# Loading the second layer's weight matrices in 192 KB pieces into fixed places

## Chip, cores and metric

The kernel runs on one core of one Trainium2 chip. The metric is the device time of one execution in microseconds (us); shown are the single runs and their median. The page and the trace come from one further, profiled execution.

## The reference, cut to what matters

Two graph layers follow each other on 128 graphs of 64 nodes with 768 features, in float32. The weights of the second layer, Wq, Wk, Wv and Wf, are what the change concerns.

```python
x = _layernorm(x + _L0_gnn_ref(x, adj, W, b, w_src, w_dst, H_w, H_b))       # 12 heads of 64
x = _layernorm(x + _L1_gnn_ref(x, Wq, bq, Wk, bk, Wv, bv, Wf, bf, adj))     # 6 heads of 128

# _L0_gnn_ref: h = x @ W per head; th = tanh(h)
attn = leaky(th @ w_src + (th @ w_dst).T)        # masked by adj, softmax over nodes
feat_out = elu(attn @ h + b)
gate = sigmoid(x @ H_w.T + H_b)
return gate * feat_out + (1.0 - gate) * x

# _L1_gnn_ref
q, k, v = heads(x @ Wq + bq), heads(x @ Wk + bk), heads(x @ Wv + bv)
probs = softmax(q @ k.T / sqrt(128) + bias_of(adj))
return (probs @ v) @ Wf + bf
```

## The kernel before, in words

**Products.** Every multiplication by a 768 x 768 matrix is done as a two by two block product with seven block multiplications instead of eight. Each matrix is therefore held as seven blocks of 384 x 384: W11, W21, W22, T1, T2, T3 and N4, of which four are sums and differences of weights. One matrix in SBUF is a tile of 128 partitions, seven blocks, KH = 3 slices of the contracted dimension, and 384 columns; a block is 576 KB, the matrix 4.1 MB. The products take the blocks in the order of TURNS (line 64): W11, T2, T1, W21, T3, W22, N4. `by_token` (line 274) gives tokens as rows, with the weights as the moving operand: h, g (the gate), v and o. `by_feature` (line 345) gives features as rows: q and k, 256 tokens at a time for each of 7 products.

**First layer.** The 64 token tiles of 128 are taken in 32 pairs (loop at line 794). For each pair `hidden` multiplies by w0, `gate` by h_w, and `value` by wv, the last for the pair two before. That is 21 products, one period. The rest of a tile's work (`attend`, line 574) runs over the two periods from its start: scores, softmax, a DMA transpose of the weights (`turn_weights`, line 667), whose result ACT puts together (`weights`, line 671), 24 small matmuls on each side of the graph pair (`means`, line 674, tile f_all), elu and gate, layer norm, a second DMA transpose (`turn_rows`, line 731), whose result ACT puts together (`rows`, line 735, tile x_even or zone), and sums of the transposed rows (line 749, x_sums), which `value` reads. The blocks of rows go to device memory (`away`, line 762) as operands of the second layer, and v too (line 541).

**Second layer.** `phase_b` goes through 16 quads of four tiles. For each of three f it makes queries and keys (`by_feature`), and starts `slab` (line 888), which does the scores and the softmax of two heads, turns the result by a DMA transpose (line 936, tiles s and sT; ACT copies at lines 935 and 940), multiplies by v (tile c_ps, line 952), and turns that by two more DMA transposes (line 967). `output` multiplies by wf. `last_bias` (line 854) also reads wf, before the first keys of quad 1.

**Order of work.** The kernel has a schedule of its own: class `Beat` (line 94) counts products. `product` emits one product and moves the count by one; `at` queues a piece of work for a count, `start` runs a generator whose yields are numbers of beats to wait, and `until` lets the count run on. Keys in `KEYS`, `SUMS`, `X_BLOCKS` and `MASKS` say at which beat of the period each step of `attend` and its neighbours is emitted. Emission order is the order on each engine's queue. All DMAs, transposes included, are issued by SP on one queue, in order; an SP instruction that waits holds all behind it.

**The matrices.** w0, h_w and wv are loaded at the start (`prepared`, line 187). Meanwhile `matrices` (line 437) builds the seven blocks of wq, wk and wf and writes them to device memory (`to_there`, line 209). `matrix` (line 222) brings one back: it takes the next buffer of the pool `weights` (line 169, three buffers), so that wq takes the one of w0, wk that of h_w and wf that of wv, and issues seven DMAs of 576 KB, one a beat; then it sets `ready`. In the last pair (period of 21 beats from its beat 0) wq starts behind `hidden`, wk behind `gate`. After the loop, `first_blocks` (line 820) loads seven operand blocks of quad 0, two DMAs of 192 KB each (line 334), one block a beat, beside `value(30)`; then follow queries(0, 0), keys(0, 0) and `value(31)`. wf starts at the beginning of `phase_b`.

Each wait of a generator ends 0.7 of a beat after a whole count:

```python
        def step():
            wait = next(line, None)
            if wait is not None:
                self.at(self.now + wait + 0.7, step, order)

        self.at(self.now + after + 0.7, step, order)
```

Of the kernel before, what the change touches and what calls it, by code (L numbers as in the profile page):

```python
# [30 lines left out]
F32 = mybir.dt.float32  # L31
# [8 lines left out]
P = 128  # L40
# [3 lines left out]
KH = KC // 2  # L44
HALF = D // 2
# [48 lines left out]
class Beat:  # L94
# [13 lines left out]
    def start(self, line, after=0):  # L108

        self.issued += 1  # L110
        order = self.issued

        def step():
            wait = next(line, None)
            if wait is not None:
                self.at(self.now + wait + 0.7, step, order)

        self.at(self.now + after + 0.7, step, order)

    def product(self, emit, then):  # L120
        emit()
# [18 lines left out]
def two_layers(  # L140
# [21 lines left out]
    nc = tc.nc  # L162
    n_tiles = x.shape[0] // P
    n_quads = n_tiles // 4
    n_pairs = n_tiles // 2
    beat = Beat()

    const = ctx.enter_context(tc.tile_pool(name="const", bufs=1))
    wpool = ctx.enter_context(tc.tile_pool(name="weights", bufs=3))
    dram = ctx.enter_context(tc.tile_pool(name="dram", bufs=1, space=DRAM))  # L170
    tiny = ctx.enter_context(tc.tile_pool(name="tiny", bufs=3))

    def sb(pool, shape, tag, name, bufs=None, dtype=F32):
        return pool.tile(shape, dtype, tag=tag, name=name, bufs=bufs)
# [9 lines left out]
    bq_sb = const.tile([P, H1], F32, name="bq_sb")  # L184
    bk_sb = const.tile([P, H1], F32, name="bk_sb")

    def prepared(w, name, engine):

        t = sb(wpool, [P, 7, KH, HALF], "w", name)
        blocks = w.rearrange("(k c p) (m n) -> k m p c n", k=2, p=P, m=2)  # L190
        for at, k, m in ((W11, 0, 0), (T3, 0, 1), (W22, 1, 1), (W21, 1, 0)):
            nc.sync.dma_start(t[:, at], blocks[k, m])
            yield t
        yield from sums_of_weights(engine, t)

    def sums_of_weights(engine, t):

        engine.tensor_tensor(t[:, T1], t[:, T3], t[:, W11], ALU.subtract)
        yield 1
        engine.tensor_tensor(t[:, T2], t[:, W22], t[:, T1], ALU.subtract)  # L200
        yield 1
        engine.tensor_tensor(t[:, T3], t[:, W22], t[:, T3], ALU.subtract)
        yield 1
        engine.tensor_tensor(t[:, N4], t[:, W21], t[:, T2], ALU.subtract)


    w_there = {n: dram.tile([P, 7, KH, HALF], F32, name=f"{n}_there") for n in ("wq", "wk", "wf")}
# [11 lines left out]
                nc.sync.dma_start(w_there[name][:, :, c, q * P : (q + 1) * P], t)  # L219
                yield 4  # L220

    def matrix(name):

        t = sb(wpool, [P, 7, KH, HALF], "w", f"{name}_sb")
        for at in (W11, T2, T1, W21, T3, W22, N4):
            nc.sync.dma_start(t[:, at], w_there[name][:, at])
            yield 1
        ready[f"{name}_sb"] = t


    def heads(ap, n):
        return ap.rearrange("p (h e) -> p h e", h=n)
# [21 lines left out]
    def row(w, name, pool):  # L254
        t = pool.tile([P, w.shape[0]], F32, name=name)
        nc.sync.dma_start(t, w.partition_broadcast(P))
        return t
# [16 lines left out]
    def by_token(name, blocks, w, reads):  # L274

        sums = [sb(dense[0], [P, BANK], "dense", f"{name}{i}") for i in range(3)]
        begun = set()
        for what, to, xb, wb in TURNS:
            ps = sums[to][:, 0:HALF]

            def emit():
                for c in range(KH):
                    nc.tensor.matmul(  # L283
                        ps,
                        lhsT=blocks[xb][:, c, :],
                        rhs=w[:, wb, c, :],
                        start=(c == 0 and to not in begun),
                        stop=(c == KH - 1),
                        skip_group_check=True,
                    )  # L290

            read = reads[what]
            beat.product(emit, lambda read=read, ps=ps: read(ps))
            begun.add(to)
# [101 lines left out]
    def phase_a(pa, ps_a, dst_pool):  # L396
        def x_blocks(p):

            t = in_zone(0, KC, 2, P)
            nc.sync.dma_start(t, xT[:, p])  # L400
            b = [t[:, 0:KH, 0], t[:, KH:KC, 0], t[:, 0:KH, 1], t[:, KH:KC, 1]]
            s = in_zone(2 * D, 4, KH, P)
            blocks[p] = b + [s[:, i] for i in range(4)]
            yield
            yield from sums_of_tokens(nc.gpsimd if p else nc.vector, s, *b)

        def now(line, steps):
            for _ in range(steps):
                t = next(line, None)
            return t  # L410

        x_line = x_blocks(0)
        w0_line = prepared(w0, "w0_sb", nc.vector)
        now(x_line, 1)
        w0_sb = now(w0_line, 4)
        now(x_line, 1)
# [1 line left out]
        now(x_line, 1)  # L418
        now(w0_line, 3)
        w_dst_sb = row(w_dst, "w_dst_sb", pa)  # L420
        h_w_line = prepared(h_w, "h_w_sb", nc.vector)
        h_w_sb = now(h_w_line, 4)
        beat.start(h_w_line)
        w_src_sb = row(w_src, "w_src_sb", pa)
# [3 lines left out]
        nc.vector.tensor_scalar(b0_sb, b0_sb, 1.0, None, ALU.add)  # L428
        less_one = const.tile([P, 1], F32, name="less_one")
        nc.vector.memset(less_one, -1.0)  # L430
        wv_line = prepared(wv, "wv_sb", nc.gpsimd)
        wv_sb = now(wv_line, 4)
        beat.start(wv_line, 10)
        for to, vector in ((bv_sb, bv), (bq_sb, bq), (bk_sb, bk)):
# [16 lines left out]
        def part(name):  # L451
            return sb(pa, [P, HALF], "part", name, 8)

        def tiles_of(p):
            return 4 * (p // 2) + p % 2, 4 * (p // 2) + p % 2 + 2


        def hidden(p, A, B):
            u = {}

            def h_of(S, m):
                return S["h"][:, 6 * m : 6 * m + 6, 0:E0]

            def th_of(S, m):
                return heads(S["th"][:, m * HALF : (m + 1) * HALF], 6)

            def half_done(S, m):
                beat.soon(lambda: nc.scalar.activation(th_of(S, m), h_of(S, m), AF.Tanh))

            def p1(ps):  # L470
                u[1] = part(f"h1_{p}")
                nc.scalar.copy(u[1], ps)

            def p6(ps):
                u[2] = part(f"h2_{p}")
                nc.vector.tensor_tensor(u[2], u[1], ps, ALU.add)

            def p2(ps):
                nc.scalar.copy(h_of(A, 0), heads(ps, 6))
                nc.scalar.activation(th_of(A, 0), heads(ps, 6), AF.Tanh)  # L480

            def p5(ps):
                u[3] = part(f"h3_{p}")
                nc.vector.tensor_tensor(u[3], u[1], ps, ALU.add)

            def p7(ps):
                nc.vector.tensor_tensor(h_of(B, 1), heads(u[3], 6), heads(ps, 6), ALU.add)
                half_done(B, 1)

            def p4(ps):  # L490
                nc.vector.tensor_tensor(h_of(B, 0), heads(u[1], 6), heads(ps, 6), ALU.add)
                nc.scalar.activation(th_of(B, 0), h_of(B, 0), AF.Tanh)

            def p3(ps):
                nc.vector.tensor_tensor(h_of(A, 1), heads(u[2], 6), heads(ps, 6), ALU.add)
                nc.scalar.activation(th_of(A, 1), h_of(A, 1), AF.Tanh)  # L496

            by_token(f"h_{p}_", blocks[p], w0_sb, dict(P1=p1, P2=p2, P3=p3, P4=p4, P5=p5, P6=p6, P7=p7))
# [295 lines left out]
        for p in range(n_pairs):  # L794
            ta, tb = tiles_of(p)
            A = {"t": ta, "p": p, "side": 0}
            B = {"t": tb, "p": p, "side": 1}
            begin = p * period
            for side, S in enumerate((A, B)):
                S.update(h=h_of_tile[(2 * p + side) % 3], th=th_d[side], g=gates[side])  # L800
            masks(p, A, B, begin)
            for S in (A, B):
                attend(S, begin)
            sums_of_pair(p, begin)
            if p + 1 < n_pairs:
                line = x_blocks(p + 1)
                for key in X_BLOCKS:
                    beat.at(begin + key, lambda line=line: next(line, None))
            beat.until(lambda: beat.now == begin)
            hidden(p, A, B)  # L810
            if p + 1 == n_pairs:
                beat.start(matrix("wq"), 1)
            gate(p, A, B)
            blocks.pop(p)
            if p + 1 == n_pairs:
                beat.start(matrix("wk"), 6)
            if p > 1:
                value(p - 2)

# [26 lines left out]


    def phase_b(pb, ps_b):
        beat.start(matrix("wf"), 1)
        bf_sb = row(bf, "bf_sb", pb)  # L850

        def last_bias():
# [206 lines left out]
        def at_place(q, f):  # L1059

            return (None, 0, 1)[f]

        load(Q)
        for q in range(n_quads + 1):
            for f in range(3):
# [4 lines left out]
                if before and at_place(q, f) is not None:  # L1070
                    i = at_place(q, f)
# [15 lines left out]
    with (  # L1087
        tc.tile_pool(name="pb", bufs=1) as pb,
        tc.tile_pool(name="ps_b", bufs=1, space=PSUM) as ps_b,
        tc.tile_pool(name="dense_b", bufs=5, space=PSUM) as dense_b,  # L1090
        tc.manual_schedule(),
    ):
        dense[:] = [dense_b]
        phase_b(pb, ps_b)
# [47 lines left out]
```

## Time and profile before

| What | us |
|---|---|
| three runs | 2899.72, 2900.83, 2900.92 |
| their median | 2900.83 |
| the profiled execution | 2900.76 |
| its span, first to last instruction | 2898.9 |
| PE busy in it | 2835.3 (98%) |
| beat 0 of the last pair (first product of h) | at 1349.2 |
| end of v of the last pair, start of the second phase's products | at 1459.9 |

In the profile, PE is TensorE's matmuls, PEld its weight loads, DVE VectorE, ACT ScalarE, POOL GpSimd, and SPq the queue of SyncE, which issues the DMAs. A line of waits reads: engine, tile and line that waited, what released it, us in total, times, longest. A table by stretches gives, for each engine, busy us and the number of instructions, then the granted clock of TensorE, the mean busy share of the 16 DMA engines (overlapping packets can take it above 1), and GB/s. A timeline gives start, length, engine, line and operation; of an SPq line the length is that of the issue, not of the transfer. The page's list of DMA issues gives the median from issue to landing:

| DMA | KB each | us to landing |
|---|---|---|
| wq_sb, wk_sb, wf_sb from device memory, 7 each | 576 | 7.1, 5.7, 9.8 |
| zone<-ops_there (operand blocks), 224 | 192 | 4.7 |
| transposes th_d<-bc_e, elu_turned<-xg_parts, s<-sT | | 3.8, 5.6, 3.0 |

### The profile page before, as it was taken

What the parts mean: (1) busy time and instruction counts of PE and PEld (TensorE: products, weight loads), DVE (VectorE), ACT (ScalarE), POOL (GpSimd) and SP (SyncE); (2) the same over time, 40 slices, a digit from 0 to 9 for tenths busy, and PEclk for the clock granted to TensorE, in tenths of its full rate; (3) what the DMA queues carried; (4) which work ended last, traced back from release to release, by engine and by line L of the source; (5) the groups of instructions that cost most, each with busy time, mean ns of one, the idle gap of its engine ahead of it and who ended that gap; (6) DMA issues with size and microseconds to landing.
All of it is one profiled execution on the core that took longest, in us unless ns stands there. A gap on an engine that the chain in (4) does not pass through costs nothing.

```text
span 2898.9 us, 42338 instructions
## 1 busy us (share of the span) xinstructions
PE 2835.3 (98%) x15586; PEld 1923.0 (66%) x15586; DVE 1919.0 (66%) x3555; ACT 1326.2 (46%) x1594; POOL 1190.4 (41%) x1106
## 2 busy tenths in 40 slices
PE   7899999999999999999799999999999999999998
PEld 4555555555555555555577787777777777877775
DVE  6999999999999999999534444444444444444444
ACT  2555655656556656555423333333333333333332
POOL 5667767766766656665201111211112212122113
PEclk8999999999999999999999999999999999999999
DMA  6667767677675665666863445443544434543432
GB/s 186 168 190 199 198 194 199 197 194 195 188 208 163 181 167 160 180 169 182 244 166 92 103 127 123 108 117 86 123 115 120 111 91 113 130 123 100 110 96 78
DMA packets 664302, 434.29 MB, mean 150 GB/s; under 512 B 442144, under 2 KB 607648, under 8 KB 664096
## 3 DMA queue, kind: packets, MB, share of 16 engines
q1 hardware_dynamic: 664096, 431.59, 55.7%
q8 instruction: 123, 2.02, 0.3%
q14 instruction: 83, 0.68, 0.1%
HBM read 199.07 MB, written 132.32 MB: 114 GB/s over the span
## 4 chain that ended last, share of the span: by engine, by line
PE 72%; DMA 1%; DVE 1%; SPq 1%; ACT 0%; issue 0%; POOL 0%; POOLq 0%; DVEq 0%; ACTq 0%
PE o L283 15%; PE q L379 15%; PE k L379 15%; PE v L283 8%; PE h L283 7%; PE g L283 7%; PE s_ps L896 2%; PE c_ps L952 2%; PE f_all L681 1%; DMA s<-sT 0%; PE bias_ps L858 0%; DMA th_d<-bc_e 0%; DMA zone<-ops_there 0%; DMA elu_turned<-xg_parts 0%; DVE st L300 0%
## 5 line engine op out<-in xcount | busy, mean ns | idle before, releaser
L283 PE MATMUL h<-w_sb,zone 128*128 128x384 f32 x1344 | 463.4, 498 | 28.0 <-DMA zone<-in_xT 9.1
L283 PE MATMUL g<-h_w_sb,zone 128*128 128x384 f32 x1344 | 452.4, 491 | 3.1 <-DVE g L523 3.1
L379 PE MATMUL q<-zone,wq_sb 128*128 128x256 f32 x2016 | 450.9, 381 | 1.1 <-DVE v L566 0.7
L379 PE MATMUL k<-zone,wk_sb 128*128 128x256 f32 x2016 | 446.2, 381 | 0.5 <-ACT k_u L359 0.5
L379 PEld LDWEIGHTS q<-zone,wq_sb 128*128 128x128 f32 x2016 | 382.4, 191 | 62.2 <-issue 2.0
L999 POOL TENSOR_TENSOR y<-y,bf_sb 128x768 f32<-128x768 f32 x64 | 114.8, 1813 | 745.9 <-DMA y<-x_there 637.2
L379 PEld LDWEIGHTS k<-zone,wk_sb 128*128 128x128 f32 x2016 | 380.6, 190 | 56.6 <-issue 5.0
L283 PEld LDWEIGHTS h<-w_sb,zone 128*128 128x128 f32 x1344 | 253.1, 193 | 216.0 <-issue 39.4
L283 PEld LDWEIGHTS g<-h_w_sb,zone 128*128 128x128 f32 x1344 | 250.0, 190 | 183.3 <-DVE g L523 19.2
L283 PE MATMUL o<-wf_sb,sc 128*128 128x384 f32 x768 | 268.0, 493 | 2.8 <-DVE sc L252 2.8
L283 PE MATMUL v<-wv_sb,x_sums 128*128 128x384 f32 x768 | 260.3, 489 | 5.3 <-DVE x_sums L252 5.3
L307 POOL TENSOR_TENSOR rs<-rs,power 128x1 f32<-128x1 f32 x128 | 71.1, 556 | 437.4 <-DVE rs L305 437.4
L283 PEld LDWEIGHTS v<-wv_sb,x_sums 128*128 128x128 f32 x768 | 146.4, 191 | 108.5 <-DVE x_sums L252 6.5
L601 POOL TENSOR_TENSOR bc_e<-th_d,w_dst_sb 128x768 f32<-128x768 f32 x64 | 118.9, 1858 | 236.4 <-ACT th_d L496 130.3
L283 PEld LDWEIGHTS o<-wf_sb,sc 128*128 128x128 f32 x768 | 144.0, 191 | 100.0 <-DVE sc L252 3.8
L283 PE MATMUL o<-wf_sb,cT 128*128 128x384 f32 x576 | 203.3, 489 | 0.5 <-ACT cT L962 0.5
L1012 POOL TENSOR_TENSOR o<-o,y 128x384 f32<-128x384 f32 x96 | 107.4, 1120 | 185.6 <-issue 85.7
L966 ACT COPY parts<-c_ps 128x1024 uint16<-128x1024 uint16 x94 | 95.4, 1015 | 148.5 <-PE c_ps L952 148.5
L283 PEld LDWEIGHTS o<-wf_sb,cT 128*128 128x128 f32 x576 | 107.9, 190 | 72.6 <-issue 2.6
L672 ACT COPY bc_e<-th_d 128x1536 uint16<-128x1536 uint16 x64 | 123.6, 1931 | 59.2 <-DMA th_d<-bc_e 57.6
L597 POOL TENSOR_TENSOR xg_parts<-xg_parts,zone 128x768 f32<-128x768 f32 x64 | 116.5, 1820 | 56.4 <-issue 34.3
L725 ACT ACTIVATE mix<-mix,rs 128x768 f32<-128x768 f32 x64 | 65.3, 1020 | 158.8 <-POOL rs L308 158.8
(159 smaller groups left out, 4587.5 us busy)
## 6 DMA issues: line engine op xcount, KB each, us to landing
zone<-ops_there SPq DMA_DIRECT2D x224, 192.0 KB, 4.7
zone<-in_xT SPq DMA_DIRECT2D x32, 768.0 KB, 4.6
zone<-in_x SPq DMA_DIRECT2D x64, 384.0 KB, 3.9
bc_e<-there SPq DMA_DIRECT2D x128, 192.0 KB, 3.3
x_there<-mix SPq DMA_DIRECT2D x64, 384.0 KB, 3.9
ops_there<-x_sums SPq DMA_DIRECT2D x32, 768.0 KB, 3.2
v_there<-v SPq DMA_DIRECT2D x128, 192.0 KB, 2.4
v<-v_there SPq DMA_DIRECT2D x128, 192.0 KB, 3.9
```

The costliest lines, as they stand in the source:

```text
L283: nc.tensor.matmul(ps, lhsT=blocks[xb][:, c, :], rhs=w[:, wb, c, :], start=(c == 0 and to not in begun), stop=(c == KH - 1), skip_group_ch ...
L307: nc.gpsimd.tensor_tensor(rs[:, 0:1], rs[:, 0:1], power, ALU.pow)
L379: nc.tensor.matmul(ps, lhsT=w[:, wb, c, f * P : (f + 1) * P], rhs=blocks[xb][:, c, :], start=(c == 0 and to not in begun), stop=(c == KH - 1),
L597: nc.gpsimd.tensor_tensor(xg, xg, xs, ALU.mult)
L601: nc.gpsimd.tensor_tensor(bc, th, w_dst_sb, ALU.mult)
L672: nc.scalar.copy(halves(e), by_halves(d))
L725: nc.scalar.activation(f, f, AF.Identity, bias=rs[:, 1:2], scale=rs[:, 0:1])
L896: nc.tensor.matmul(s_ps[b * N : (b + 1) * N, i, r, :], lhsT=qT[:, r, at], rhs=kT[:, r, at], start=True, stop=True,)
L952: nc.tensor.matmul(c_ps[cols, r, i, :], lhsT=sT[rows, i, cols], rhs=v_of, start=True, stop=True)
L966: nc.scalar.copy(by_halves(parts), halves(c_ps[:, r].rearrange("p i t -> p (i t)")))
L999: nc.gpsimd.tensor_tensor(y, y, bf_sb, ALU.add)
L1012: nc.gpsimd.tensor_tensor(u[k], u[of], y[:, m], ALU.add)
```

## The change

The pool `weights` goes. Three tiles of the pool `const` take its place, and a table says which matrix lies in which: w0 and then wq in the first, h_w and then wk in the second, wv and then wf in the third. `matrix` splits each of its seven DMAs by the slice c of the contracted dimension, into 21 DMAs of 192 KB with 1536 contiguous bytes for each partition (before 4608), and takes the number of beats between two of them as an argument: 1.2 for wq and wk, 1 for wf. In the last pair wq starts at beat 0, ahead of `hidden`, so that its first piece is emitted at beat 1.7 (before 8.7), and wk's first at beat 8.7 (before 20.7); wf's first comes at beat 2.7 of the second phase (before 1.7). `Beat.start` keeps the time of each step itself, so that waits need not be whole beats. Nothing else is changed.

```diff
-        def step():
+        def step(time):
             wait = next(line, None)
             if wait is not None:
-                self.at(self.now + wait + 0.7, step, order)
-
-        self.at(self.now + after + 0.7, step, order)
+                self.at(time + wait, lambda: step(time + wait), order)
+
+        time = self.now + after + 0.7
+        self.at(time, lambda: step(time), order)
...
-    wpool = ctx.enter_context(tc.tile_pool(name="weights", bufs=3))
...
+    places = [const.tile([P, 7, KH, HALF], F32, name=f"w_{i}") for i in range(3)]
+    place = {"w0": 0, "h_w": 1, "wv": 2, "wq": 0, "wk": 1, "wf": 2}
+
     def prepared(w, name, engine):
 
-        t = sb(wpool, [P, 7, KH, HALF], "w", name)
+        t = places[place[name]]
...
-    def matrix(name):
-
-        t = sb(wpool, [P, 7, KH, HALF], "w", f"{name}_sb")
+    def matrix(name, gap):
+
+        t = places[place[name]]
         for at in (W11, T2, T1, W21, T3, W22, N4):
-            nc.sync.dma_start(t[:, at], w_there[name][:, at])
-            yield 1
+            for c in range(KH):
+                nc.sync.dma_start(t[:, at, c], w_there[name][:, at, c])
+                yield gap
         ready[f"{name}_sb"] = t
...
             beat.until(lambda: beat.now == begin)
+            if p + 1 == n_pairs:
+                beat.start(matrix("wq", 1.2), 1)
+                beat.start(matrix("wk", 1.2), 8)
             hidden(p, A, B)
-            if p + 1 == n_pairs:
-                beat.start(matrix("wq"), 1)
             gate(p, A, B)
             blocks.pop(p)
-            if p + 1 == n_pairs:
-                beat.start(matrix("wk"), 6)
...
     def phase_b(pb, ps_b):
-        beat.start(matrix("wf"), 1)
+        beat.start(matrix("wf", 1), 2)
```

More of the change, by code (lines that the diff above doesn't have):

```diff
@@ L412, in phase_a @@
         x_line = x_blocks(0)
-        w0_line = prepared(w0, "w0_sb", nc.vector)
+        w0_line = prepared(w0, "w0", nc.vector)
         now(x_line, 1)
@@ L420, in phase_a @@
         w_dst_sb = row(w_dst, "w_dst_sb", pa)
-        h_w_line = prepared(h_w, "h_w_sb", nc.vector)
+        h_w_line = prepared(h_w, "h_w", nc.vector)
         h_w_sb = now(h_w_line, 4)
@@ L430, in phase_a @@
         nc.vector.memset(less_one, -1.0)
-        wv_line = prepared(wv, "wv_sb", nc.gpsimd)
+        wv_line = prepared(wv, "wv", nc.gpsimd)
         wv_sb = now(wv_line, 4)
```

## The prediction

> **What bounds the kernel now.** I read the page first: which engine is full, and for how long it is not.
>
> ```profile
> span 2898.9 us, 42338 instructions
> PE 2835.3 (98%) x15586; PEld 1923.0 (66%) x15586; DVE 1919.0 (66%) x3555; ACT 1326.2 (46%) x1594; POOL 1190.4 (41%) x1106
> ```
>
> PE is busy all but 63.6 us, and the change adds and removes no matmul, so it can only win idle PE time, or slow matmuls that follow idle. Next, PE's waits. Some 31 us end before beat 0 of the last pair (the start-up: h waits for inputs and weights), 4 us come in the last stretch. Between 1385 and 1500 us, where the second layer's matrices arrive, stand these:
>
> ```profile
> PE f_all L681 <- ACT bc_e L672: 7.6, 1, 7.6
> PE v L283 <- DVE x_sums L252: 5.3, 2, 3.8
> PE c_ps L952 <- ACT sT L940: 4.9, 1, 4.9
> PE v L283 <- ACT x_even L737: 1.7, 1, 1.7
> ```
>
> All four end on a copy that itself waits for a DMA transpose. The table by stretches, with PE, PEld, DVE, ACT and POOL busy, then clock, DMA share and GB/s, shows why the transposes are late:
>
> ```profile
> 1349.00:1390.00 41.00, 40.99 (x217) 23.90 (x216) 37.21 (x66) 20.69 (x23) 22.22 (x18) 1.00 0.71 206
> 1390.00:1423.00 33.00, 21.93 (x110) 12.68 (x108) 16.23 (x30) 13.36 (x12) 8.51 (x7) 0.92 1.11 298
> 1472.00:1480.00 8.00, 8.00 (x39) 7.04 (x38) 1.86 (x5) 1.57 (x3) 0.00 (x0) 1.00 1.02 408
> ```
>
> The DMA engines are full from 1390 to 1423 us, and not before. The chain that ended last names the steps (start, length, what), and the SP queue's timeline shows what stands in front of each transpose:
>
> ```profile
> 1402.88 4.41 DMA wk_sb<-wk_there
> 1407.30 6.71 DMA zone<-ops_there
> ...
> 1414.08 8.90 DMA th_d<-bc_e
> ...
> 1472.81 11.70 DMA s<-sT
> ```
>
> ```profile
> 1467.91 4.22 SPq L226 DMA_DIRECT2D wf_sb<-wf_there  x7
> 1472.81 6.34 SPq L936 DMA_TRANSPOSE s<-sT  x1
> ```
>
> So two congested places: A, the end of the first layer (wq, wk, and the operand blocks of L334 together), and B, the start of the second (seven wf blocks of 576 KB straight before the first sT transpose, which lands after 11.7 us; the page's median for s<-sT is 3.0). In SP's timeline [...] (wk at 1402.88 releases L334 at 1407.30), so a DMA that lands late also holds the issue of later ones.
>
> [...] the s<-sT transpose lands only after 4.1 MB of wf. [...] after 7.6 idle us the 48 f_all matmuls took 1.58 us against 0.86 elsewhere, and the stretches 1420 to 1430 and 1480 to 1490 show a granted clock of 0.66.
>
> **The change, part by part.** Times are against the profiled execution, 2900.76 us (span 2898.9 and 1.9 around it); the median shown, 2900.83, is 0.07 off, nothing here. A beat is one product: about 2.05 us in the first layer with its extras (43 us for 21), 1.3 us in the second. Beat 0 of the last pair is 1349.2 us.
>
> *Beat.step with a time of its own, tiles in const instead of a pool*: no instruction. All other lines wait whole beats and start at a fraction of 0.7; floor plus wait plus 0.7 is then time plus wait, so nothing else moves. Cost 0.
>
> *Order on PE*: wq is ready at 1.7 + 21 x 1.2 = 26.9 (before 15.7), wk at 8.7 + 25.2 = 33.9 (27.7), wf at 2.7 + 21 = 23.7 of the second phase. They are asked for at beats 28, 35 and 35 (last_bias). No until-loop turns longer, so PE's order is kept. Each old block was read before its piece's turn (W11 of w0 at product 0, its pieces at 1.7 to 4.1), so no new wait on PE; the wait of 0.8 us of the first L226 on the last h goes.
>
> *More waits on PE*: the first queries and keys wait for 42 pieces instead of 14 blocks, all long landed. No row shows such a wait alone; between 0 and 28 x 0.05 us (an "issue" step of the chain) = 1.4 us; I take 0[...]. Not below 0.
>
> *SP issues*: 21 pieces at about 0.53 us (a pair of 192 KB L334 issues took 1.06 us) against 7 blocks at 0.43. Before the last turn_weights of the pair (beat 25.15) 34 pieces are queued against 12 blocks, 22 more, 22 x 0.53 = 11.7 us of SP. From 1349 to 1415 SP's timeline holds 47.8 us of issuing in 66, part of which is blocked issue. Beats 14.3 to 21.5 get 12 pieces, 6.4 us of some 15, so stretch by stretch they fit. I take 0; ends 0 and 11.7.
>
> *Rate of the pieces*: no stretch moves such pieces alone. The 14 L334 loads (512-byte rows at one end) ran at 255 GB/s, the wf blocks at 408 to 424. A line through 512 bytes at 300 GB/s (the level of its second half) and 4608 at 424 GB/s (per engine 27 and 174 ns) gives 64 ns for 1536, 386 GB/s. I take 386; ends 255 and 408.
>
> *A, DMA work before and after 1390 us (beat 20.5 or so)*: before, 6.3 wq blocks (3.7 MB, 9.1 us at 408) lay ahead of 1390, and of the 12 that precede the last transpose 17.3 - 9.1 = 8.2 us fell into the full stretch. After, 16 wq and 10 wk pieces (5.1 MB, 13.2 us at 386) lie ahead of 1390; there is room: 41 - (0.71 x 41 - 9.1) = 21.0 us. Only 8 pieces (1.6 MB, 4.1 us) are left. So 4.1 us less work, at a share of 1.11 3.7 us sooner: f_all's stall goes from 7.6 to 3.9. Ends: 1.8 at 255 GB/s with no room to spare (20 of 21.0), 0 if they back up; 7.6 if the shorter queue also cuts the landings before it (there<-dst took 6.1 us, th_d's side 0 7.0 against a median of 3.8). The slow matmuls after it cost 0.72 (f_all) and 0.88 (q, 7.55 against 6.67); I take half, 0.8. For v (5.5 us, both waits) I take 0: ahead of the first elu transpose 4 pieces replace 2 blocks (0.4 MB less), ahead of the second 6 replace 1 (0.6 MB more). Ends -2 and +4. A together: 3.7 + 0.8 = 4.5.
>
> *B*: the transpose is emitted at beat 7.7, after pieces 2.7 to 7.7: six of 192 KB, 1.2 MB against 4.1. Issued from 1467.9 they are done by 1472. If none had drained at 1472.81: 3.1 us at 386, and 3.0 for the transpose, 1478.9, and ACT's first L940 0.8 later, 1479.7; PE asks at 1480.5. So the stall goes, at both ends: 4.94, and the slow c_ps (1.98 against 1.03) and q (3.99 against 2.79), 7.1 in all. The 15 later pieces move 192 KB in 1.3 us, beside 120 GB/s: 270, below 386. Late next would be the second slab's sT (its copy ended 2.1 us before c_ps at 1508.1); if that cover is gone, 1 to 2 us come back.
>
> Sum: 4.5 + 7.1 = 11.6; 2900.76 - 11.6 = **2889.2 us**.
>
> **Rivals.** *B alone* (chance 0.17): the work of A is only dealt out differently, pieces hold back v as much as they spare f_all. For it: the full stretch and v's end at +0.6 MB. 2900.8 - 7.1 = 2893.7. *All stalls go* (0.20): with the load even, latencies fall to their medians. For it: f_all never waited over 0.2 us in earlier pairs. 1.74 + 3.78 + 7.56 + 4.94 = 18.0, clock 1.8 (v after 3.78) + 1.6 + 2.2 = 5.6: 2877.2, or some 2881 with part of it. Against it: the engines stay near full. *No change* (0.08): the landings are set by other traffic (operand blocks 2.7 MB, ops_there 1.3 MB); about 2900. *Slower* (0.08): the SP queue becomes the bound. It issues in order and stands still in waits (there<-dst 12.2 us in four), so the 22 extra issues end up ahead of the last th_d transpose instead of in SP's gaps: f_all 11.7 us later, B's 7.1 still won: 2905.4. It decides from 7.1 / 0.53 = 13 of the 22 on. Against it: by stretches SP has room.
>
> **Chances.** The forecast has 0.47. A time is told from no change at about 0.2%, 5.8 us. Faster: 0.47 + 0.20 + 0.13 of B alone = 0.80; same: the other 0.04, no change 0.08, 0.03 of slower = 0.15; slower 0.05. The range: 2878 (all stalls) to 2896 (B alone with 2 us given back), which leaves out no change, slower and the end of "all": some 0.2.
>
> **What would show it.** Right: no PE wait on L940 near 1475, s<-sT landing within 6 us; f_all's wait 2 to 5 us; v's about 5; DMA share 0.8 to 0.95 before 1390. Wrong: DMA share above 1 before 1390 with longer v waits (pieces slower than 386 GB/s); SP issuing without a gap before L669 (slower); a PE wait on c_ps at the second slab; or PE idle before q or k on a zone load.

## The result, and the profile after

The changed kernel takes 2890.8 us (median of 7 runs) against 2900.8 (7 runs): a ratio of 0.9966, with a 95% interval of 0.9955 to 0.9978. That is 10.0 us faster, where 11.6 were forecast (2889.2, range 2878 to 2896). In later runs beside three experiments the same kernel had a median of 2893.3 against 2900.5, ratio 0.9969 (0.9958 to 0.9981). Most single runs of a kernel lie within 3 us of their median, some 6 us off (in e6 below, three of twelve lie 7 to 23 us above it), so two kernels whose medians differ by 3 us aren't told apart below.

From the page of the changed kernel: the same matmuls, a shorter span, and PE still busy 98% of it.

```profile
span 2889.1 us, 42394 instructions
PE 2833.0 (98%) x15586; PEld 1921.6 (67%) x15586; DVE 1920.1 (66%) x3555; ACT 1327.3 (46%) x1594; POOL 1190.5 (41%) x1106
```

PE's waits between 1385 and 1500 us (engine, tile, line, releaser; us in all, times, longest):

```profile
PE f_all L686 <- ACT bc_e L677: 7.0, 1, 7.0
PE v L288 <- DVE x_sums L257: 3.8, 2, 2.3
```

Of the four waits before, c_ps (4.9) is gone and so is v's on x_even (1.7); v's on the sums is 3.8 instead of 5.3. But f_all, the largest, has hardly changed: 7.0 against 7.6. The table by stretches (length, the five engines' busy time, clock, DMA share, GB/s):

```profile
1349.00:1390.00 41.00, 40.99 (x217) 23.89 (x216) 37.31 (x64) 22.64 (x25) 23.33 (x19) 1.00 0.77 218
1390.00:1423.00 33.00, 23.67 (x150) 14.50 (x152) 17.28 (x32) 14.80 (x14) 8.51 (x7) 0.88 1.14 301
1472.00:1480.00 8.00, 8.00 (x65) 6.75 (x64) 1.87 (x4) 2.87 (x4) 0.00 (x0) 1.00 0.78 196
```

The share before 1390 rose only from 0.71 to 0.77, and the stretch after it is as full as ever (1.14). In this execution beat 0 comes 1.1 us later; over the same distance from it, 1350 to 1391, the share is 0.79, and in the last 10 us of that it is 1.02 already (0.79 before). The start of the second phase is relieved: 196 GB/s where the wf blocks had moved 408. SP's timeline there, and the answer for the transpose's line:

```profile
1464.77 3.54 SPq L231 DMA_DIRECT2D w<-wf_there  x6
1470.12 1.57 SPq L940 DMA_TRANSPOSE s<-sT  x1
1471.73 3.43 SPq L231 DMA_DIRECT2D w<-wf_there  x7
```

```profile
DMA to landing us min/median/max: 4.5/4.5/4.5
```

Six pieces instead of seven blocks stand ahead of the s<-sT transpose. It lands after 4.5 us instead of 11.7, at 1474.6, and its copy is ahead of PE's c_ps at 1477.7.

### The profile page after: what moved, and what is told of

Same layout as the page of the kernel before. It is cut to its first block, busy times and chain, and to the rows that moved or that the text cites. A ratio compares the mean times of both kernels' runs of the same rounds, so it can differ in the third digit from the quotient of the medians.

```text
span 2889.1 us, 42394 instructions
## 1 busy us (share of the span) xinstructions
PE 2833.0 (98%) x15586; PEld 1921.6 (67%) x15586; DVE 1920.1 (66%) x3555; ACT 1327.3 (46%) x1594; POOL 1190.5 (41%) x1106
## 4 chain that ended last, share of the span: by engine, by line
PE 50%; DMA 1%; DVE 1%; ACT 0%; issue 0%; SPq 0%; POOL 0%; POOLq 0%; DVEq 0%; ACTq 0%
PE o L288 15%; PE k L384 15%; PE q L384 15%; PE s_ps L900 2%; PE c_ps L956 2%; PE v L288 1%; DMA elu_turned<-xg_parts 1%; PE bias_ps L862 0%; DMA th_d<-bc_e 0%; DMA zone<-ops_there 0%; ACT x_even L742 0%; DVE st L305 0%; DMA v<-v_there 0%; DVE x_sums L257 0%; DVE sc L257 0%
## 5 line engine op out<-in xcount | busy, mean ns | idle before, releaser
L288 PE MATMUL h<-w,zone 128*128 128x384 f32 x1344 | 463.7, 498 | 28.7 <-DVE h L481 9.4
L288 PE MATMUL g<-w,zone 128*128 128x384 f32 x1344 | 452.4, 491 | 3.0 <-DVE g L528 3.0
L384 PE MATMUL q<-zone,w 128*128 128x256 f32 x2016 | 449.7, 381 | 1.5 <-DVE v L571 0.7
L384 PE MATMUL k<-zone,w 128*128 128x256 f32 x2016 | 446.2, 381 | 0.5 <-ACT k_u L364 0.5
L384 PEld LDWEIGHTS q<-zone,w 128*128 128x128 f32 x2016 | 381.5, 190 | 62.1 <-issue 1.8
L384 PEld LDWEIGHTS k<-zone,w 128*128 128x128 f32 x2016 | 380.6, 190 | 56.6 <-issue 5.0
L288 PEld LDWEIGHTS h<-w,zone 128*128 128x128 f32 x1344 | 253.2, 193 | 216.8 <-issue 39.2
L288 PEld LDWEIGHTS g<-w,zone 128*128 128x128 f32 x1344 | 250.0, 190 | 183.3 <-DVE g L528 19.1
L288 PE MATMUL o<-w,sc 128*128 128x384 f32 x768 | 268.0, 493 | 2.8 <-DVE sc L257 2.8
L288 PE MATMUL v<-w,x_sums 128*128 128x384 f32 x768 | 260.2, 489 | 3.8 <-DVE x_sums L257 3.8
L288 PEld LDWEIGHTS v<-w,x_sums 128*128 128x128 f32 x768 | 146.5, 191 | 106.9 <-DVE x_sums L257 5.1
L1016 POOL TENSOR_TENSOR o<-o,y 128x384 f32<-128x384 f32 x96 | 107.3, 1119 | 184.4 <-issue 83.0
L602 POOL TENSOR_TENSOR xg_parts<-xg_parts,zone 128x768 f32<-128x768 f32 x64 | 116.6, 1821 | 52.9 <-issue 34.3
```

The costliest lines, as they stand in the source:

```text
L288: nc.tensor.matmul(ps, lhsT=blocks[xb][:, c, :], rhs=w[:, wb, c, :], start=(c == 0 and to not in begun), stop=(c == KH - 1), skip_group_ch ...
L384: nc.tensor.matmul(ps, lhsT=w[:, wb, c, f * P : (f + 1) * P], rhs=blocks[xb][:, c, :], start=(c == 0 and to not in begun), stop=(c == KH - 1),
L602: nc.gpsimd.tensor_tensor(xg, xg, xs, ALU.mult)
L1016: nc.gpsimd.tensor_tensor(u[k], u[of], y[:, m], ALU.add)
```

## The experiments

All were profiled once. To compare them I cut each profiled execution at three matmuls: the first h of the last pair, the first q of the second phase, and the first bias_ps. A is the first interval (the end of the first layer), B the second. The start-up before the first cut differs by chance, 1347.8 to 1351.2 us between executions, and what follows B is 1377.6 to 1380.3 in all of them. v, f_all and c_ps are PE's waits between 1385 and 1500 us; v holds two multiplications by wv, that of the last pair but one (5.5 of the 7.0 before) and, after f_all, that of the last pair.

| Run | median us | ratio to before, 95% interval | A | v | f_all | B | c_ps |
|---|---|---|---|---|---|---|---|
| before | 2900.8 | 1 | 110.7 | 7.0 | 7.6 | 59.6 | 4.9 |
| e8 before again | one run, 2899.4 | | 109.2 | 5.1 | 7.5 | 60.1 | 4.6 |
| changed | 2890.8 | 0.9966 (0.9955 to 0.9978) | 106.5 | 3.8 | 7.0 | 53.0 | 0 |
| e12 changed again | 2893.3 | 0.9969 (0.9958 to 0.9981) | 104.7 | 2.0 | 8.4 | 53.1 | 0 |
| e1 only wf | 2893.8 | 0.9976 (0.9968 to 0.9985) | 108.3 | 4.1 | 9.4 | 52.2 | 0 |
| e2 only wq, wk | 2898.2 | 0.9990 (0.9982 to 0.9998) | 106.9 | 3.6 | 7.6 | 59.1 | 4.2 |
| e3 blocks, early | 2893.4 | 0.9973 (0.9961 to 0.9984) | 109.3 | 6.0 | 6.8 | 53.3 | 0 |
| e10 the same, short rows | 2893.3 | 0.9975 (0.9965 to 0.9986) | 108.0 | 4.2 | 5.4 | 53.2 | 0 |
| e9 pieces, late | 2892.8 | 0.9972 (0.9961 to 0.9983) | 109.4 | 3.9 | 8.7 | 52.8 | 0 |
| e4 pause | 2889.5 | 0.9963 (0.9950 to 0.9975) | 106.4 | 6.7 | 3.5 | 52.8 | 0 |
| e5 wk late | 2889.2 | 0.9959 (0.9945 to 0.9973) | 105.5 | 7.5 | 0 | 52.8 | 0 |
| e11 three groups | 2889.8 | 0.9962 (0.9948 to 0.9975) | 105.3 | 5.8 | 3.6 | 52.9 | 0 |
| e6 GpSimd's queue | 2892.1 | 0.9981 (0.9965 to 0.9997) | 107.3 | 3.8 | 4.5 | 52.2 | 0 |
| e7 without wk | 2883.6 | 0.9938 (0.9923 to 0.9953) | 100.4 | 4.6 | 0 | 52.5 | 0 |

My theory was that two separate stalls are relieved, each set by the bytes that SP has queued ahead of a transpose. The rivals: only B counts; or SP's issues, or other traffic, set A.

**The two halves alone.** e1 leaves wq and wk as they were, e2 wf.

```diff
         for at in (W11, T2, T1, W21, T3, W22, N4):
+            if name in whole:
+                nc.sync.dma_start(t[:, at], w_there[name][:, at])
+                yield gap
+                continue
             for c in range(KH):
...
# e1: whole = ("wq", "wk")
-                beat.start(matrix("wq", 1.2), 1)
-                beat.start(matrix("wk", 1.2), 8)
             hidden(p, A, B)
+            if p + 1 == n_pairs:
+                beat.start(matrix("wq", 1), 1)
             gate(p, A, B)
             blocks.pop(p)
+            if p + 1 == n_pairs:
+                beat.start(matrix("wk", 1), 6)
# e2: whole = ("wf",)
-        beat.start(matrix("wf", 1), 2)
+        beat.start(matrix("wf", 1), 1)
```

> Only wf is brought in as 21 pieces; wq and wk keep their seven blocks and their old times. Theory (what is won is two separate stalls, about 7 us at the start of the second phase and about 4 us at the end of the first): some 2894, c_ps without a wait, f_all and v waiting 7.6 and 5.5 us as before. Rival (spreading wf also needs the earlier finish of the first layer, or moves its stall on): above 2896, or a wait on c_ps of the second slab.

> Only wq and wk are brought in as pieces, early; wf is seven blocks at beat 1.7 of the second phase. Theory: some 2897.5, with s<-sT landing after 11 to 12 us and a c_ps wait of about 5 us. Rival (pieces of wq and wk win nothing by themselves; the change of the v wait is a shift of one stall into another): 2900 to 2901.

e1 wins 6.8 us of its 2900.6, e2 2.4 (0.6 to 5.2 by its interval). Together 9.2, where the whole wins 10.0 in one set of runs and 7.2 in the other (e12): two gains that add up within that spread, two thirds or more of them in B. e2's waits still hold c_ps, and SP's timeline in it the old picture, blocks straight ahead of a transpose whose issue alone takes 6.3 us:

```profile
PE f_all L692 <- ACT bc_e L683: 7.6, 1, 7.6
PE c_ps L962 <- ACT sT L950: 4.2, 1, 4.2
PE v L294 <- DVE x_sums L263: 3.6, 2, 2.1
```

```profile
1465.99 4.31 SPq L233 DMA_DIRECT2D w<-wf_there  x7
1471.38 6.30 SPq L946 DMA_TRANSPOSE s<-sT  x1
```

**The kernel before, and the changed one, once more**, unedited:

> The kernel before once more, for a second profile of it: how far its stages differ between two executions. Start-up to beat 0 of the last pair 1348 to 1351 us, from there to the second phase's first product 110 to 111 us if that stretch is steady, 108 if the shorter one of the run with only wf changed was chance; the second phase to bias_ps 59 to 60.

> The changed kernel once more, beside the three others on the same chip: 2890 to 2892, and a second profile of it. From beat 0 of the last pair to the second phase's first product 106 to 107 us, f_all's wait 6 to 7 us.

A with the old wq and wk is 110.7, 109.2 and (e1) 108.3 us, with the new ones 106.5, 104.7 and (e2) 106.9: mean 109.4 against 106.0. One execution can be 1.3 us off its mean, so a single A says little below that.

By time alone the rival "B alone", 2893.7 us by the prediction, isn't excluded: e12's median is 2893.3 and e1's 2893.8. Against it stand e2, whose interval just leaves out zero, and A, whose three values with the new wq and wk all lie below the three with the old. What A follows is seen in these times, in us after beat 0 of the last pair (PE there: when PE reaches f_all):

| wq and wk | second elu transpose landed | last th_d transpose issued | landed | PE there |
|---|---|---|---|---|
| old (before, e8, e1) | 46.0 to 47.9 | 63.7 to 64.9 | 72.0 to 73.8 | 64.6 to 68.2 |
| new (changed, e12, e2) | 43.8 to 44.5 | 60.8 to 62.0 | 68.8 to 70.1 | 62.4 to 64.7 |
| e3 blocks, early | 46.8 | 62.7 | 72.0 | 67.2 |
| e10 the same, short rows | 45.9 | 63.2 | 70.8 | 67.4 |
| e9 pieces, late | 44.5 | 63.4 | 71.6 | 64.9 |
| e6 GpSimd's queue | 42.7 | 58.7 | 70.1 | 67.6 |
| e4 pause | 48.7 | 61.8 | 70.6 | 69.1 |
| e11 three groups | 45.4 | 60.0 | 68.3 | 66.8 |
| e5 wk late | 43.0 | 57.1 | 62.4 | 65.0 |
| e7 without wk | 39.7 | 56.7 | 62.9 | 66.7 |

The elu transpose leads to the sums that v waits for, the th_d transpose to f_all.

**What in A wins: early, or small?** e3 keeps the changed start and pace but brings whole blocks; e9 brings pieces at the old start and pace; e10 is e3 with the matrices stored so that a block comes in rows of 1536 bytes.

```diff
# e3: whole = ("wq", "wk")
-                beat.start(matrix("wq", 1.2), 1)
-                beat.start(matrix("wk", 1.2), 8)
+                beat.start(matrix("wq", 3.6), 1)
+                beat.start(matrix("wk", 3.6), 8)
# e9: started as in e1, and
+                beat.start(matrix("wq", 1 / 3), 1)
...
+                beat.start(matrix("wk", 1 / 3), 6)
# e10: e3, and
-    w_there = {n: dram.tile([P, 7, KH, HALF], F32, name=f"{n}_there") ...}
+    w_there = {n: dram.tile([P, KH, 7, HALF], F32, name=f"{n}_there") ...}
```

> The changed kernel with wq and wk as seven blocks of 576 KB each, in the changed kernel's place and at its pace in bytes (3.6 beats for a block, first at 1.7 and 8.7). If bytes and the time at which they are asked for decide, and not the size of a piece: 2890 to 2892. If small pieces are what lets the transposes through: 2894 or more, with a v wait of over 4 us. If the 28 added issues and the shorter packets of pieces cost: 2888 or less.

> The changed kernel with wq and wk in 21 pieces each, but started where the kernel before starts them and at its pace in bytes (a third of a beat for a piece). The first elu transpose of the pair before then has six pieces, 1.2 MB, straight ahead of it, as many bytes as two blocks. If the bytes ahead decide: it lands after about 9 us and the whole takes some 2894, as with only wf changed. If the cutting decides: it lands after 5 to 6 us, v waits 2 to 4 us, 2891.

> Early whole blocks of 576 KB, as in the run with early blocks, but with the matrices kept in device memory so that a block comes in rows of 1536 bytes instead of 4608: the number of DMAs and the bytes are those of that run, the rows those of the pieces. If the length of the rows ahead of a transpose is what makes it slow: the elu transposes land after 5 to 6 us and the whole takes about 2891. If the number of bytes or of DMAs: they land after 9 and 8 us again, 2893 to 2894.

Neither alone is seen to win anything in A: 109.3 for early blocks, 109.4 for late pieces, 108.0 for early blocks of short rows, against 108.3 to 110.7 of the old form and 104.7 to 106.9 of the new. By the medians the three are 2 to 2.6 us behind the changed kernel's first 2890.8 and level with its second 2893.3, so this is not told apart by time. The transposes do show a difference: the second elu transpose comes as late with early blocks (46.8) as before, and as soon with late pieces (44.5) as in the changed kernel, and v's wait ahead of f_all is 4.5 us in e3 and 2.4 in e9. The cutting moves v. The last th_d transpose, which A follows, is late in both (72.0, 71.6); of these forms it is clearly sooner only where pieces also come early (68.8 to 70.1). SP's timelines around the first elu transpose of the last pair but one, in e3, the changed kernel and e9:

```profile
1380.91 0.54 SPq L739 DMA_DIRECT2D x_there<-mix  x1
1381.50 0.42 SPq L233 DMA_DIRECT2D w<-wk_there  x1
1381.97 0.52 SPq L233 DMA_DIRECT2D w<-wq_there  x1
1382.60 5.17 SPq L744 DMA_TRANSPOSE elu_turned<-xg_parts  x1
```

```profile
1380.78 0.54 SPq L733 DMA_DIRECT2D x_there<-mix  x1
...
1383.48 1.85 SPq L738 DMA_TRANSPOSE elu_turned<-xg_parts  x1
```

```profile
1381.43 0.54 SPq L733 DMA_DIRECT2D x_there<-mix  x1
1382.01 3.50 SPq L231 DMA_DIRECT2D w<-wq_there  x7
1385.61 1.96 SPq L738 DMA_TRANSPOSE elu_turned<-xg_parts  x1
```

Behind two blocks the transpose holds SP for 5.2 us and lands after 9.5 (8.0 in e10); the second one in e3, also behind two blocks, holds it for only 2.2. Behind four pieces it holds SP for 1.9 and lands after 5.8, behind seven (e9) 5.7. But a landing counted from issue misleads: SP spent 3.5 us on issuing the seven pieces, in a stretch in which the engines were busy (a share of 1.00 from 1381 to 1392). Counted from x_there, the first in the row, it landed after 8.5 us with 0.8 MB of matrix between (four pieces), 9.9 with 1.4 MB (e9), and 11.2 with 1.2 MB in blocks (e3). Four pieces against seven is 1.4 us for 0.6 MB, which the bytes explain at 386 GB/s, the prediction's estimate (1.5 us). In these executions blocks are slower by more than their bytes (2.7 us more than four pieces, for 0.4 MB). Short rows change little: the first landing (8.0 against 9.5) and the held issue (4.5 against 5.2) are near what two blocks of long rows gave in e1 (8.6, 4.4). Why SP was held longer behind whole blocks stays open.

**Bytes in one queue, or bytes at all?** In e6 GpSimd issues the 14 blocks on a queue of its own, which the page lists apart with 8.26 MB.

```diff
# e3, and
-                nc.sync.dma_start(t[:, at], w_there[name][:, at])
+                nc.gpsimd.dma_start(t[:, at], w_there[name][:, at])
```

> The changed kernel with wq and wk as seven blocks each, 3.6 beats apart, issued by GpSimd on a queue of its own instead of by SP. If standing in one queue ahead of the transposes is what costs: the transposes issue and land sooner, v and f_all wait under 5 us together, 2884 or so. If the sixteen engines' bytes are what costs, whichever queue holds them: 10 us together as before and 2891 to 2894, more if issuing costs GpSimd time that v or the softmax waits for.

A is 107.3, the median 2892.1. SP issues the last th_d transpose 2.5 us sooner, no longer behind the blocks in its queue, but it lands after 11.4 us instead of 8.4, and so no sooner (70.1 us after beat 0, 69.6 in the changed kernel). f_all waits less (4.5) because PE comes later; another f_all wait of 1.6 us comes up earlier. The two elu transposes ahead of it landed after 7.0 and 7.4 us too, where they took 5.8 and 5.1 in the changed kernel. So with the blocks in a second queue the transposes were late as well. My reading, not shown apart, is that both queues want the same sixteen engines, whose share was 1.09 from 1390 to 1423. That SP's issues are not the limit is likely but not shown apart: 28 fewer in e3 and 42 fewer in e6 made neither faster than the changed kernel, but both have blocks in place of pieces.

**Where the stall goes when the bytes are moved.** e4, e5 and e11 give other start times to the pieces; e7 leaves wk's DMAs out, so that keys are made with the gate's weights. In e4, e5 and e11 the pace is a list, one gap for each piece.

```diff
# e4
+                beat.start(matrix("wq", [0.9] * 21), 1)
+                beat.start(matrix("wk", [1.2] * 8 + [8] + [0.6] * 12), 8)
# e5
+                beat.start(matrix("wq", [0.9] * 21), 1)
+                beat.start(matrix("wk", [0.42] * 21), 25.3)
# e11
+                beat.start(matrix("wq", [0.45] * 21), 1)
+                beat.start(matrix("wk", [0.1] * 3 + [6.55] + [0.5] * 4 + [5.6] + [0.5] * 12), 10.85)
# e7
+                if name != "wk":
                     nc.sync.dma_start(t[:, at, c], w_there[name][:, at, c])
```

> The changed kernel with another spacing: wq at 0.9 of a beat from 1.7 (done at 19.7), nine pieces of wk from 8.7 to 18.3, none until 26.3, then the other twelve at 0.6 of a beat. No matrix bytes are asked for in the five beats ahead of the last transpose of the first layer's weights. If the bytes queued ahead of it set f_all's wait: it falls from 7.0 to 3 or 4 us, 2887 or so, if v does not wait longer for the 1.2 MB more that now come before it (then 2889). If the operand blocks and the other traffic set it, or SP's queue: 7 us as before, 2891.

> The changed kernel with wq at 0.9 of a beat from 1.7 (done at 19.7) and all of wk only behind the last transpose of the first layer's weights, from beat 26.0 at 0.42 of a beat. Theory (the bytes asked for ahead of a transpose set its wait, whether v's or f_all's): v waits about 2 to 3 us, f_all about 3, in all 5 us less than the changed kernel in these two; wk's 4.1 MB then stand before the next elu transposes, and v of the last pair or k gives 3 to 6 us back: 2887 to 2891. Rival (SP's queue or other traffic): v and f_all wait 10 us together as before.

> wq at 0.45 of a beat from 1.7 (done at 10.7); wk in three groups: four pieces at 11.6 to 11.9 (the engines idle there while SP waits for there), five at 18.4 to 20.4 (behind the last elu transpose of the pair before), twelve from 26.0 at half a beat (behind the last th_d transpose). Theory (place matters, bytes ahead of each transpose): f_all waits under 2 us, v 4 us in all, 4 to 6 us less than the changed kernel: 2885 to 2887. Rival (the engines are full in this stretch in any order): 2889 to 2891.

> The changed kernel without the 21 DMAs of wk; keys are made with what lies in its place (the gate's weights). It gives the price of wk's 4.1 MB in this stretch. Theory (bytes ahead of the transposes): v under 2 us and f_all 1 to 3 us of wait, some 2883 to 2885. Rival (operand blocks and stored rows fill the engines by themselves): f_all still waits over 5 us, 2888 or more.

Waits of e4, then of e5 and e7:

```profile
PE v L289 <- DVE x_sums L258: 6.3, 2, 5.9
PE f_all L687 <- ACT bc_e L678: 3.5, 1, 3.5
```

```profile
PE v L289 <- DVE x_sums L258: 4.8, 2, 2.9
PE v L289 <- ACT x_even L743: 2.7, 1, 2.7
PE q L385 <- DMA zone<-ops_there: 0.9, 1, 0.9
```

```profile
PE v L289 <- DVE x_sums L258: 4.6, 2, 3.1
```

e4 was to show that the pieces queued ahead of the last th_d transpose set f_all's wait, and the wait is halved. But the transpose landed no sooner (70.6 us after beat 0); with no piece issued in the 12 us before it, it still took 8.8 us, behind eight operand loads of 192 KB and the stored rows. The wait is shorter only because PE, held longer by v, came 4.4 us later. For this transpose the rival of e4's expectation, operand blocks and other traffic, fits.

```profile
1396.93 0.42 SPq L232 DMA_DIRECT2D w<-wq_there  x1
...
1404.54 3.26 SPq L340 DMA_DIRECT2D zone<-ops_there  x6
...
1409.58 4.16 SPq L675 DMA_TRANSPOSE th_d<-bc_e  x1
```

With wk wholly behind that transpose (e5), it landed at 62.4, and f_all doesn't wait at all. Then the pieces stand ahead of the last pair's elu transposes, as SP's timeline of e5 shows:

```profile
1420.26 3.97 SPq L232 DMA_DIRECT2D w<-wk_there  x8
1424.42 0.32 SPq L734 DMA_DIRECT2D x_there<-mix  x1
1424.90 2.30 SPq L232 DMA_DIRECT2D w<-wk_there  x4
1427.30 2.06 SPq L739 DMA_TRANSPOSE elu_turned<-xg_parts  x1
```

ACT had the first of those rows ready at 1420.5; SP reached the transpose at 1427.3, and v of the last pair and its sums wait 2.7 and 1.9 us. f_all came 6.7 us sooner after beat 0 than in the changed kernel (65.0 against 71.7), the end of A only 1.0 (105.5 against 106.5). e11, meant to have the best of both, missed: f_all 3.6 and v 5.8, and 2889.8 us, the time of its rival. Its early burst of wq held back the there<-dst round trip (issued at 1374.2 against 1369.9), and with it the first elu transpose (1387.8 against 1383.5). The three medians are 1 to 1.6 us under the changed kernel's first and some 4 under its second; by their intervals they aren't told apart from it. e7 prices wk: without its 4.1 MB A is 100.4, 6.1 us less, and f_all has no wait. Some 7 to 10 us of the median (2883.6 against 2890.8 and 2893.3) is, as an estimate, the most that a better place for wk could win. v's wait, expected under 2 us, is 4.6, though the second elu transpose landed 4.8 us sooner: ACT had copied its rows by 1393.8, but VectorE (DVE), busy with the softmax, came to the sums at 1395.4 and took 2.9 us for them (1.2 in the changed kernel).

```profile
1395.36 1.62 DVE L258 SCALAR_TENSOR_TENSOR x_sums<-x_even 128x384 f32<-128x384 f32 x1
```

In the changed kernel DVE stood idle 0.9 us for the copy of the rows just before these sums. So in e7 v's wait has a second cause close behind the transpose, and the earlier landing did not win all of it.

The theory stands, then, for B as a whole, and in A for taking wk out of the transposes' way (e5, e7). The pieces straight ahead of a transpose don't set its landing by themselves (e4: none in the 12 us before it, and 8.8 us to landing).

## Why the prediction was right, step by step

**B, 7.1 us: right.** e1 won 6.8; B fell from 59.6 to 53.0. Stall and slow matmuls both went: in the changed kernel the c_ps matmuls took 1.10 us, where 1.98 had followed the wait, and the clock granted in the 6 us from their start was 1.00, where it had been 0.65. The transpose landed 17.8 us after the second phase's first product (1474.6 - 1456.8), before the 19.0 (1478.9 - 1459.9) that was taken as the latest. No wait came back at the second slab. Whether the fewer bytes ahead of the transpose (1.2 MB against 4.1) or the smaller transfers did it, no run separates for B.

**A, 4.5 us: near in sum, wrong in its parts, and the nearness partly luck.** In the profiled pair A fell by 4.2, in the mean of three by 3.4; e2 won 2.4 (0.6 to 5.2). The prediction gave 3.7 to f_all and "For v (5.5 us, both waits) I take 0". It was the other way: v's wait in value of the last pair but one fell from 5.5 to 2.35 (inside its ends of -2 and +4), f_all's from 7.6 to 7.0. The step that failed is v's: "ahead of the second 6 replace 1 (0.6 MB more)" took the bytes straight ahead of the second transpose as what delays it. With 0.6 MB more ahead it landed sooner, 44.5 us after beat 0 (1389.70 + 5.1) instead of 47.9: 1.0 by an earlier issue, the first one holding SP for 1.9 us instead of 5.1, and 2.4 by a shorter way from issue to landing (5.1 against 7.5). In the three executions of each form that way is 4.7 to 5.1 with pieces and 7.5 to 7.7 with blocks, in e9 4.7, in e3 and e10 7.8 and 6.9; in the mean the issue is hardly sooner (39.2 us after beat 0 against 39.4). Why a transpose behind blocks took that much longer stays open.

The step on f_all came near in size, not by its route. The transpose landed 73.8 us after beat 0 before (1414.08 + 8.9 - 1349.2) and 69.6 after, 4.2 sooner, where 3.7 were forecast. From the changed kernel's chain:

```profile
1407.27 4.25 DMA zone<-ops_there
1411.60 8.37 DMA th_d<-bc_e
```

The forecast had 26 pieces ahead of 1390 and 8 left. SP's timeline has 22 by the same distance from beat 0 (1391.1) and 12 between there and the transpose: 6.1 us at 386 GB/s, so that the same sum gives 1.9 us, not 3.7. And 3.6 of the 4.2 us are an earlier issue (61.3 against 64.9), only 0.5 a quicker landing. By the chains, what releases the issue is an operand load eight places ahead in SP's queue, which landed after 4.25 us instead of 6.71; the upper end of the forecast had named such landings, its middle had left them out. How much of this is fewer bytes and how much smaller pieces stays open: e3 and e9 each have only part of it.

PE, less held by v, arrived 3.6 sooner too (64.7 us after beat 0 against 68.2), so its wait barely shrank. In these executions the end of A follows the landing, wherever that comes after PE, whatever share of the way there PE spends waiting on v. That is why the sum held; it would not have been right to add v's 3.2 us to f_all's.

**Clock, 0.8 us in A: did not come.** f_all's wait stayed at 7 us, and what came after it was as slow as before: over the 9 us from f_all's start the granted clock was 0.83 against 0.82, f_all's 48 matmuls took 1.58 us in both, and the q matmuls after them 7.47 against 7.55. The prediction set busy times against distances of starts here (1.58 with 0.86, 7.55 with 6.67); like with like, the slow matmuls cost 0.65 and 0.81 us, a tenth less each.

**Rate, 386 GB/s, and room before 1390:** the room was smaller than computed. By the same distance from beat 0 some 0.9 MB more had moved (227 GB/s against 206 over 41 us), where 1.4 were forecast, and the last 10 us were full (1.02). Nothing shows the pieces slower than blocks in the engines; four against seven pieces agree with that rate.

**SP's issues, waits on PE, Beat's own time: 0, right** as far as seen. *Slower* had SP's 22 extra issues on the path; e3 has none of them and is no faster. *B alone* is answered by A and the landings above, not by the time. *All stalls go* did not happen: f_all's wait is gone only in e7, without wk, and in e5, which gives most of it back.

## What to carry to other kernels

In a kernel like this one, where prefetches share a queue and its engines with small transfers on the critical path, list what stands ahead of each of those, and count the time to the last landing from a fixed point, not from its issue: from the issue, four and seven pieces ahead look alike here (5.8 and 5.7 us), from x_there they do not (8.5 and 9.9). A wait that shrinks upstream of a later one was no gain of its own here: v's fell by 3.2 us, and f_all's still took 7.0. What counted was whether the later release moves (the landing of th_d's transpose, 4.2 us sooner). Bringing wf in pieces spread over the second phase's products paid, where the engines had time free: their share from 1472 to 1480 was 0.78 with the pieces, and B fell by 6.6 us. In the full stretch at the end of the first layer (a share of 1.01 to 1.14 in the changed kernel, e4, e5 and e11) moving bytes from one deadline to the next gained nothing over the changed kernel that the times tell apart. A halved wait alone, as in e4 (3.5 us against 7.0, with the landing no sooner), shows nothing won.

## What the runs showed of the hardware that was not expected

The issue of a DMA transpose held SP's queue for 2.2 to 5.2 us straight behind two 576 KB blocks and for 6.3 behind seven (in the kernel before and in e2); straight behind four to seven 192 KB pieces for 1.3 to 2.7, and for 1.3 just ahead of beat 0, before these matrices. But the last th_d transpose held it for 3.8 to 4.2 in the changed kernel, e4 and e11 too, behind operand blocks of 192 KB and stored rows of 192 to 768 KB: that the matrices came in pieces did not make this hold short. With transposes in the same queue, three transfers in place of one, with rows a third as long, cost nothing that was seen: the medians are 2890.8 and 2893.3 us with wq and wk in pieces, 2893.4 with the same start and pace in blocks (e3).
